# Moving the last feed-forward's norm, gate and first routing choice into the causal attention's slots (a four-block transformer stack on one Trainium2 core)

## The chip, the cores and the metric

The kernel runs on one core of a Trainium2 chip. A core has five engines with their own instruction queues: TensorE (PE, matrix products, with a separate row for its weight loads), VectorE (DVE), ScalarE (ACT), GpSimd (POOL) and SyncE (SP, which here only issues DMA transfers). SBUF is the on-chip memory, PSUM the banks that PE writes, DRAM the memory outside. The metric is the device time of one execution in microseconds (us); lower is better.

## The reference

The input is 8 rows of 512 tokens with 256 features. Six blocks are added to it one after the other, each on the layer norm of the running sum x:

```python
x = x + 0.5 * _L0_ffn_ref(_layernorm(x), ...)
x = x + _L0_attn_ref(_layernorm(x), ...)
x = x + 0.5 * _L0_ffn_ref(_layernorm(x), ...)
x = x + 0.5 * _L1_ffn_ref(_layernorm(x), ...)
x = x + _L1_attn_ref(_layernorm(x), ...)
x = x + 0.5 * _L1_ffn_ref(_layernorm(x), ...)
```

The change touches the last three. `_L1_attn_ref` is causal attention with 16 heads of 16 features, whose scores are scaled by an embedding of the distance (clipped at 16). `_L1_ffn_ref` is a mixture of 8 experts with a shared expert beside them:

```python
scores = sigmoid(x @ gate_W) * route_scale
topk_scores, topk_idx = top_k(scores, 2)
topk_w = topk_scores / topk_scores.sum(-1)
h = gelu(x @ W1[e] + b1[e]);  y = h @ W2[e] + b2[e]     # for each expert e
out = sum over the two chosen e of topk_w * y  +  gelu(x @ Ws1 + bs1) @ Ws2 + bs2
```

## The kernel before

x stays in SBUF as eight tiles `c.x[b]`, one per row of 512 tokens, each as 4 groups of 128 tokens on the partitions. All data is fp32, and the profile counts two matmul records for each fp32 product.

**The mixture (`l1_ffn`, called as "f3" ahead of the attention and as "f4" behind it).** For each row, `norm` (L994) normalises the four groups on ACT into a tile `xn`, SP stores it to a DRAM tensor (`f_xn` in the profile), and POOL adds half the shared expert's last bias to x (L998). `turn` (L1005) transposes the row on PE in two halves, each copied from its bank into `xnT`; `gate` (L1013) multiplies `xnT` with the gate's weights into the logits `lg`. `share` is the shared expert: a product with `ws1` (L1024), a gelu into `hs` (L1027), two products with `ws2` (L1033), each added to x by DVE (L1037). It reads the same `xnT`, so five of these tiles are kept. `choose(h)` routes one half of the rows (h = 0: rows 0 to 3; h = 1: rows 4 to 7): a sigmoid on ACT (L1088), the two best experts, and each token's place in a list sorted by expert and padded to 39 tiles of 128 tokens. A long series of small DVE operations, one pair of counting products (L1113, L1114), eight groups of four products that build the table of tokens (L1209), and one for the bias (L1230) do it. `lists` works through the 78 tiles of both halves: POOL gathers 128 tokens by index out of `f_xn` (L1246, `xe`), PE transposes them (L1254), ACT copies the expert's weights (L1284, `we`), PE multiplies (L1272), ACT takes the gelu (L1278, `h`), PE multiplies again (L1262), DVE adds the bias (L1264) and SP stores the tile (`f_y`). `fetch` (L941) gathers a token's two results, and `add` (L950) adds them to x with their weights.

These functions are Python generators. Each `yield` ends a piece of work, and the caller interleaves the pieces: `together` steps several generators in turn, `step` one. The order so written is kept on PE, DVE, ACT and POOL; on SP, in this function, a scheduler places the transfers. A call first runs `rows` up to the gate of row 3, then `choose(0)` together with the rest of `rows` (rows 4 to 7 and the shares of rows 0 to 3), then `lists`, with the other four shares, `choose(1)` and a second stream beside it. For f3 that second stream brings rows 0 and 1 to the attention; for f4 it fetches and stores rows 0 to 3. The last fetches of f4 follow behind the lists.

**The attention (`l1_attn`).** `attend` writes out by hand the order of all five engines, SP among them, as a series of slots: 32 groups (8 rows of 4 groups of heads), 8 slots each, so row b begins at slot 32 b. In a slot PE forms one pair of score products for finding the maxima (L1569, L1574), and for the group 12 slots back the products to be weighed (L1647, L1654, L1659), which ACT turns by an exponential into `pt` (L1663); every other slot PE sums them with the values (L1677, `o`). The score banks ("s", three of them) are taken twice in a slot. Everything else uses one further bank, "mm": norm and projections of the coming row, and the end of the finished one. These are placed by the list `pieces` of slot offsets and by `put`. The end of a row is `inverse` (reciprocal of the sums), `over` (spread to all partitions by way of DRAM), `scale` (L1526), and twice `finish` (product with Wo, L1533) and `add` (L1541), at offsets 48 to 63, so that for row 7 it comes after the last scores. The rows 2 to 7 come in from f3 by `bring` and `take` in the slots ahead.

The names and lines of this section and of the profile are those of the kernel before.

Of the kernel before, what the change touches and what calls it, by code (L numbers as in the profile page):

```python
# [921 lines left out]
def l1_ffn(c, k_, tag, keep, cut_row, beside):  # L922
# [4 lines left out]

# [6 lines left out]
    xn_d = keep["dram"].tile([NTOK, D], F32, name=f"{tag}_xn")  # L934
# [19 lines left out]
    with ExitStack() as ctx:  # L954
        rp = ctx.enter_context(tc.tile_pool(name=f"{tag}_rows", bufs=2))
        rt = ctx.enter_context(tc.tile_pool(name=f"{tag}_turned", bufs=5))
        hp_ = ctx.enter_context(tc.tile_pool(name=f"{tag}_half", bufs=1))
        sp = ctx.enter_context(tc.tile_pool(name=f"{tag}_small", bufs=2))
        ep = ctx.enter_context(tc.tile_pool(name=f"{tag}_e", bufs=3))
        wp = ctx.enter_context(tc.tile_pool(name=f"{tag}_we", bufs=4))  # L960
        xp = ctx.enter_context(tc.tile_pool(name=f"{tag}_xe", bufs=5))
        ps4 = ctx.enter_context(tc.tile_pool(name=f"{tag}_ps4", bufs=4, space=PSUM))
        ps = ctx.enter_context(tc.tile_pool(name=f"{tag}_ps", bufs=2, space=PSUM))
        ps1 = ctx.enter_context(tc.tile_pool(name=f"{tag}_ps1", bufs=1, space=PSUM))
        mv = hp_.tile([P, NA, 2], F32, name="mv")
        rstd = hp_.tile([P, NA], F32, name="rstd")
        shift = hp_.tile([P, NA], F32, name="shift")
        lgs = [hp_.tile([P, COUNT[h], NE1], F32, name=f"lg{h}") for h in range(2)]
        part_of = [{}, {}]
        xn, xnT = {}, {}  # L970

        def bank():
            return ps4.tile([P, T], F32, name="m")


        def stats(b):
            for i in range(NT):
                st = sp.tile([P, 6], F32, name="st")
                nc.vector.bn_stats(out=st, in_=c.x[b][:, i, :])
                nc.vector.bn_aggr(out=mv[:, b * NT + i, :], in_=st)  # L980

        def deviations(b0, b1_):
            a = slice(b0 * NT, b1_ * NT)
            nc.scalar.activation(rstd[:, a], mv[:, a, 1], AF.Sqrt, bias=c.eps)
            nc.vector.reciprocal(out=rstd[:, a], in_=rstd[:, a])
            nc.vector.scalar_tensor_tensor(
                out=shift[:, a], in0=mv[:, a, 0], scalar=-1.0, in1=rstd[:, a], op0=ALU.mult, op1=ALU.mult
            )

        def norm(b):  # L990
            xn[b] = rp.tile([P, NT, D], F32, name="xn")
            for i in range(NT):
                n = b * NT + i
                nc.scalar.activation(  # L994
                    xn[b][:, i, :], c.x[b][:, i, :], AF.Identity, bias=shift[:, n : n + 1], scale=rstd[:, n : n + 1]
                )
            nc.sync.dma_start(xn_d[b * T : (b + 1) * T, :].rearrange("(i p) d -> p i d", p=P), xn[b])
            nc.gpsimd.tensor_tensor(c.x[b], c.x[b], k_.bs2.unsqueeze(1).to_broadcast([P, NT, D]), ALU.add)  # L998

        def turn(b, kc):  # L1000
            if kc == 0:
                xnT[b] = rt.tile([P, KC, T], F32, name="xnT")
            m = bank()
            for i in range(NT):
                nc.tensor.transpose(m[:, i * P : (i + 1) * P], xn[b][:, i, kc * P : (kc + 1) * P], c.ident)  # L1005
            (nc.scalar.copy if kc == 0 else nc.vector.tensor_copy)(xnT[b][:, kc, :], m)

        def gate(b):
            h = int(b >= cut_row)
            m = bank()[:, : NT * NE1]  # L1010
            for i in range(NT):
                for kc in range(KC):
                    nc.tensor.matmul(  # L1013
                        m[:, i * NE1 : (i + 1) * NE1], lhsT=xnT[b][:, kc, i * P : (i + 1) * P],
                        rhs=k_.gate_w[:, kc, :], start=(kc == 0), stop=(kc == KC - 1),
                    )
            i0 = (b - R[h].start) * NT
            nc.scalar.copy(lgs[h][:, i0 : i0 + NT, :], m.rearrange("p (i e) -> p i e", e=NE1))


        def share(b):
            m = bank()
            for kc in range(KC):
                nc.tensor.matmul(m, lhsT=k_.ws1[:, kc, :], rhs=xnT[b][:, kc, :], start=(kc == 0), stop=(kc == KC - 1))  # L1024
            del xnT[b]
            hs = hp_.tile([P, T], F32, name="hs")
            nc.scalar.activation(hs, m, AF.Gelu, bias=k_.bs1)  # L1027
            yield
            for i2 in range(2):
                m = bank()  # L1030
                for j in range(2):
                    i = 2 * i2 + j
                    nc.tensor.matmul(  # L1033
                        m[:, j * D : (j + 1) * D], lhsT=hs[:, i * P : (i + 1) * P], rhs=k_.ws2, start=True, stop=True
                    )
                xs = c.x[b][:, 2 * i2 : 2 * i2 + 2, :]
                nc.vector.scalar_tensor_tensor(  # L1037
                    out=xs, in0=m.rearrange("p (j d) -> p j d", j=2), scalar=0.5, in1=xs, op0=ALU.mult, op1=ALU.add
                )
                yield  # L1040

        def rows():

            stats(0)
            deviations(0, 1)
            norm(0)
            for b in range(1, cut_row):
                stats(b)
            deviations(1, cut_row)
            yield  # L1050
            for b in range(NB + 1):
                if b < NB:
                    turn(b, 0)
                    yield
                if b:
                    gate(b - 1)
                    yield b - 1
                if b < NB:
                    turn(b, 1)
                    yield  # L1060
                if b + 1 < NB:
                    if b < cut_row:
                        n = len(R[1])
                        for e in R[1][max(0, b - 1) * n // (cut_row - 1) : b * n // (cut_row - 1)]:
                            stats(e)
                    if b + 1 == cut_row:
                        deviations(cut_row, NB)
                    norm(b + 1)
                    yield
                if cut_row <= b < NB:  # L1070
                    yield from share(b - cut_row)

        def shares():
            for b in range(NB - cut_row, NB):
                yield from share(b)


        def choose(h):
            t, lg, n_, n0, tiles = part_of[h], lgs[h], COUNT[h], R[h].start * NT, TILES[h]
            wide = [P, n_, NE1]  # L1080
            a = slice(n0, n0 + n_)

            def new(name, shape, dtype=F32, own=False):
                return hp_.tile(shape, dtype, name=f"{name}{h}" if own or COUNT[0] != COUNT[1] else name)

            yield
            score = new("score", wide)
            nc.scalar.activation(score, lg, AF.Sigmoid)  # L1088
            nc.vector.tensor_scalar_mul(score, score, k_.rscale)
            revw = k_.rev.unsqueeze(1).to_broadcast(wide)  # L1090
            top = new("top", [P, 2, n_])
            hot = [new(f"hot_{k}_", wide) for k in range(2)]
            tmp = new("tmp", wide)
            left = score
            for k in range(2):
                nc.vector.tensor_reduce(out=top[:, k, :], in_=left, axis=AX.X, op=ALU.max)
                nc.vector.tensor_tensor(tmp, left, top[:, k, :].unsqueeze(2).to_broadcast(wide), ALU.is_equal)
                yield
                nc.vector.tensor_tensor(tmp, tmp, revw, ALU.mult)
                first = new(f"first_{k}_", [P, n_])  # L1100
                nc.vector.tensor_reduce(out=first, in_=tmp, axis=AX.X, op=ALU.max)
                yield
                nc.vector.tensor_tensor(hot[k], revw, first.unsqueeze(2).to_broadcast(wide), ALU.is_equal)
                yield
                if k == 0:
                    left = new("left", wide)
                    nc.vector.scalar_tensor_tensor(
                        out=left, in0=hot[0], scalar=-3e38, in1=score, op0=ALU.mult, op1=ALU.add
                    )
# [16 lines left out]
            )  # L1126

            yield

            def running(u, n, inner, name):  # L1130

                s = 1
# [753 lines left out]
```

## Time and profile before

| what | us |
|---|---|
| median of 3 runs (3315.8 to 3321.88) | 3318.16 |
| the profiled execution | 3327.53 |
| its span, from first to last instruction | 3325.7 |
| PE busy in the span | 2783.5 (84%) |
| DVE / ACT / POOL busy | 1593.6 / 1637.5 / 1657.5 |
| f3: from its first statistics to its first list tile | 2026 to 2140 |
| f3: its lists | 2140 to 2312 |
| attention, up to its last product | 2312 to 2975 |
| last row's end and f4 up to its first list tile | 2975 to 3108 |
| f4: first list / second list | 3108 to 3203 / 3203 to 3276 |
| f4: last fetches and stores | 3276 to 3326 |

The mean granted clock of PE over the span is 0.91 of full speed. A stage's share of busy time is an average; which engine sets a stage's length is read from the waits inside it. Idle time of an engine that nobody waits for costs nothing. Ends of matmuls are modelled, so that a matmul's row may reach a little over the start of the next.

### The profile page before, as it was taken

To read this page: it belongs to the slowest core of one execution; us is meant where nothing else is said; L and a number is where in the kernel's file an instruction comes from. 1 tells how busy PE (TensorE), PEld (TensorE's weight loads), DVE (VectorE), ACT (ScalarE), POOL (GpSimd) and SP (SyncE) were. 2 spreads that over 40 slices of the span, in tenths; PEclk is the share of its full clock that TensorE was granted. 3 is DMA by queue.
4 is the path that set the end of the run, shared out by engine and by line. 5 is a ranking of instruction groups with operands and counts; after the bars stand their busy time and mean duration, and the time that the engine had idled before them with its cause. 6 is when DMAs were issued, how large, how long until landed. Compare 5 with 4: busy or idle time off the path is not lost.

```text
span 3325.7 us, 53835 instructions
## 1 busy us (share of the span) xinstructions
PE 2783.5 (84%) x20313; PEld 1997.7 (60%) x20313; DVE 1593.6 (48%) x3764; ACT 1637.5 (49%) x2593; POOL 1657.5 (50%) x1285
## 2 busy tenths in 40 slices
PE   6599999888888887468999996887999999977872
PEld 5589898733343443368989885665555555545752
DVE  8311111177777777292111113675656565545653
ACT  4133333379998999342333333266444444433451
POOL 3244444378888888243444442255635453422366
PEclk9699999899999999788999996799899999986896
DMA  6599999523555666766999983153001010001264
GB/s 228 175 305 305 308 305 301 171 51 37 82 62 76 84 84 93 104 219 200 306 302 308 301 274 109 37 146 110 25 23 32 21 33 15 15 23 51 79 174 147
DMA packets 373490, 475.88 MB, mean 143 GB/s; under 512 B 93800, under 2 KB 334320, under 8 KB 356848
## 3 DMA queue, kind: packets, MB, share of 16 engines
q1 hardware_dynamic: 335024, 401.63, 43.0%
q0 software_dynamic: 38208, 70.81, 9.5%
q8 instruction: 161, 2.64, 0.3%
q14 instruction: 97, 0.79, 0.1%
HBM read 379.42 MB, written 88.47 MB: 141 GB/s over the span
## 4 chain that ended last, share of the span: by engine, by line
PE 41%; ACT 13%; DVE 10%; DMA 7%; issue 5%; POOL 3%; SPq 1%; ACTq 0%; DVEq 0%; POOLq 0%
PE hp L303 7%; PE yp L310 7%; ACT ub L666 4%; DMA band_d<-e 2%; ACT ud L666 2%; PE s L1569 2%; PE yp L1262 2%; PE o L1677 2%; PE s L1654 2%; DVE ub L655 2%; PE s L1647 2%; PE mm L1424 2%; PE yp L1272 2%; PE s L1574 1%; DMA xe<-f_xn,tok_i 1%
## 5 line engine op out<-in xcount | busy, mean ns | idle before, releaser
L307 ACT ACTIVATE hT<-hp,b1T 128x128 f32<-128x128 f32 x1024 | 375.5, 367 | 616.1 <-PE hp L303 583.5
L303 PE MATMUL hp<-xeT,w 128*128 128x128 f32 x4096 | 562.3, 281 | 23.8 <-DVE xeT L296 22.3
L303 PEld LDWEIGHTS hp<-xeT,w 128*128 128x128 f32 x4096 | 529.1, 193 | 68.7 <-DVE xeT L296 29.9
L661 POOL TENSOR_TENSOR ud<-dk,dq 128x2048 f32<-128x2048 f32 x128 | 533.6, 4199 | 68.6 <-PE do L677 36.6
L310 PE MATMUL yp<-w,hT 128*128 128x256 f32 x2048 | 507.4, 381 | 0.0
L312 DVE TENSOR_TENSOR y<-yp,b 128x256 f32<-128x256 f32 x128 | 54.4, 425 | 846.1 <-PE yp L310 546.5
L310 PEld LDWEIGHTS yp<-w,hT 128*128 128x128 f32 x2048 | 360.6, 191 | 32.7
L655 DVE SCALAR_TENSOR_TENSOR ub<-bk,relb,bq 128x512 f32<-128x512 f32 x512 | 345.1, 740 | 5.5 <-PE bo L677 5.5
L1663 ACT ACTIVATE pt<-s 128x1024 f32<-128x1024 f32 (+3 forms) x256 | 180.1, 705 | 281.6 <-PE s L1659 222.0
L666 ACT ACTIVATE ud<-ud 128x2048 f32<-128x2048 f32 x128 | 244.8, 1913 | 24.5 <-POOL ud L661 24.3
L666 ACT ACTIVATE ub<-ub 128x2048 f32<-128x2048 f32 x128 | 245.6, 1918 | 6.8 <-DVE ub L655 6.6
L286 POOL PARTITION_BROADCAST b<-b2r x128 | 82.0, 645 | 332.8 <-DVE y L312 312.8
L1246 POOL DMA_INDIRECT xe<-f_xn,tok_i x156 | 148.5, 952 | 194.3 <-PE tp L1254 96.6
L288 POOL DMA_INDIRECT xe<-xn_d,slots x128 | 129.1, 1008 | 223.5 <-PE xp L294 173.8
L314 POOL DMA_INDIRECT acc_d<-y,slots x128 | 205.8, 1608 | 68.9 <-DVE y L313 37.4
L1596 POOL TENSOR_SCALAR_AFFINE_SELECT d<-d 128x512 f32<-128x512 f32 x128 | 84.8, 662 | 291.8 <-DVE d L1586 291.3
L1586 DVE TENSOR_TENSOR d<-s,fac 128x320 f32<-128x320 f32 (+1 forms) x256 | 120.7, 472 | 218.4 <-PE s L1574 196.3
L1628 POOL TENSOR_TENSOR d<-d,nm 128x640 f32<-128x640 f32 (+1 forms) x128 | 153.6, 1206 | 62.0 <-DVE nm L1608 61.8
L1647 PE MATMUL s<-qm,kp 32*128 32x384 f32 (+2 forms) x768 | 141.0, 443 | 20.0 <-ACT pt L1663 13.5
L677 PE MATMUL bo<-ub,o_w_bond_out 128*32 128x512 f32 x1024 | 144.3, 635 | 10.7 <-ACT ub L666 10.7
L1284 ACT COPY we<-wall 128x768 f32 x156 | 129.5, 832 | 44.4 <-DVE xeT L1257 20.6
L677 PE MATMUL do<-ud,o_w_damage_out 128*32 128x512 f32 x1024 | 139.5, 616 | 10.0 <-ACT ud L666 10.0
(463 smaller groups left out, 5126.6 us busy)
## 6 DMA issues: line engine op xcount, KB each, us to landing
w<-in_L_ffn_w_dram SPq DMA_DIRECT2D x256, 1024.0 KB
f_y<-y SPq DMA_DIRECT2D x156, 128.0 KB
vb<-val_d SPq DMA_DIRECT2D x16, 1024.0 KB
pb<-band_d SPq DMA_DIRECT2D x32, 512.0 KB
xn_d<-xn SPq DMA_DIRECT2D x16, 512.0 KB
acc_d<-x SPq DMA_DIRECT2D x16, 512.0 KB
x<-acc_d SPq DMA_DIRECT2D x16, 512.0 KB
val_d<-vhalf SPq DMA_DIRECT2D x16, 512.0 KB
```

Of the source, the lines that this page charges most:

```text
L303: nc.tensor.matmul(hp[:, jj, :], lhsT=w1[:, kc, :].rearrange("c (j p) -> c j p", j=NJ0)[:, j, :], rhs=xeT[:, kc, :], start=(kc == 0), stop ...
L307: nc.scalar.activation(hT[:, j, :], hp[:, jj, :], AF.Gelu, bias=b1T[:, j, e : e + 1])
L310: nc.tensor.matmul(yp, lhsT=hT[:, j, :], rhs=w2[:, j, :], start=(j == 0), stop=(j == NJ0 - 1))
L314: nc.gpsimd.indirect_dma_start(out=acc_d[:, :], out_offset=bass.IndirectOffsetOnAxis(ap=slots[:, e : e + 1], axis=0), in_=y, in_offset=Non ...
L655: nc.vector.scalar_tensor_tensor(out=ub[:, j, :], in0=bk[:, d : d + T], scalar=relb[:, d : d + 1], in1=t["bq"], op0=ALU.add, op1=ALU.add,)
L661: nc.gpsimd.tensor_tensor(ud, win, t["dq"].unsqueeze(1).to_broadcast([P, 4, T]), ALU.subtract)
L666: nc.scalar.activation(m, m, AF.Gelu)
L677: nc.tensor.matmul(out[32 * j : 32 * (j + 1), :], lhsT=outw[name][:, k, :], rhs=m[:, j, :], start=(k == 0), stop=(k == 3),)
L1246: nc.gpsimd.indirect_dma_start(out=xe[n], out_offset=None, in_=xn_d[:, :], in_offset=bass.IndirectOffsetOnAxis(ap=part_of[h]["tok_i"][:, j ...
L1628: nc.gpsimd.tensor_tensor(d[:, i, :, lo:], d[:, i, :, lo:], pads["nm"][n % 2][:, i, :, x : x + 1].to_broadcast([P, 4, NEAR - lo]), ALU.add,)
L1647: nc.tensor.matmul(tile_[:, j, P:w_], lhsT=pads["k"][g][r, kb * P : (kb + 1) * P], rhs=grp[n]["qm"][r, (kb + 1) * P :], start=True, stop=True,
L1663: nc.scalar.activation(grp[n]["pt"][:, 2 * pair : 2 * pair + 2, :w_], tile_[:, :, :w_], AF.Exp)
```

## The change

`l1_ffn` no longer runs a whole feed-forward. It makes the tensors of one call and returns its pieces as an object, and its working memory is opened later by `open_pools`. Both calls are made ahead of the attention, so f4's pieces can be placed inside it.

- The rows 0 to 5 of f4 get statistics, norm, bias, turn and gate in slots of the attention (`more`). The norm uses the attention's tile `xn`; all turns are copied by ACT, the bias is added in four parts.
- `choose(0)` of f4 is stepped once a slot from slot 200 (`each`). Its products borrow a score bank, and the table is gathered from the bank at once (`F.prompt`).
- The last attention row's end (`rest`), the statistics to gate of rows 6 and 7, and `choose(1)` make one stream, stepped once in each of the first four list steps and twice in each later one. f4's lists begin at once behind the attention; the shares of all eight rows and the fetches run beside them.
- `gate` drops `xnT` (except for rows 6 and 7 of f4), and `share` fetches the row's `xn` again from DRAM and turns it again. This holds for f3 too. `f_xn` becomes one tensor for each half.
- Some tiles become smaller or fewer: the values' tiles hold 17 columns a head in place of 32, `raw` has one buffer, `turned` 2 (f3) or 3 (f4) in place of 5, and small tiles of `choose` are shared.

```diff
-            for i in range(NT):
-                clear.memset(v[:, i], 0.0)
-                clear.memset(v[:, i, :, BD : BD + 1], 1.0)
+            v = const.tile([P, NT, NH * VW + 32 - VW], F32, name=f"vp{n}")
+            for i in range(NT):
+                clear.memset(v[:, i, :], 1.0)
...
+    def share(b):
+        if b not in xnT:
+            xn[b] = F.rp.tile([P, NT, D], F32, name="xn")
+            nc.sync.dma_start(xn[b], stored(b))
+            yield
+            yield
+            for kc in range(KC):
+                turn(b, kc)
+                yield
...
+def run_lists(F, choices, work, second, pace):
+    for s in F.lists():
+        step(work)
+        for _ in range(pace(s)):
+            step(choices)
+        if s == F.tiles[0] - 4:
+            for _ in choices:
+                pass
+        if s > F.tiles[0] + 3:
+            step(second)
...
+            def more(put):
+                for s, b in ((96, 0), (160, 2), (224, 4)):
+                    for i, t in enumerate((-29, -28, -27, -26)):
+                        put(s + t, f4.stats, b, (i,))
+                    for i, t in enumerate((1, 1, 3, 4)):
+                        put(s + t, f4.stats, b + 1, (i,))
+                    put(s + 5, f4.deviations, b, b + 2)
+                    put(s + 6, f4.inverses, b, b + 2)
+                    for e, norms, turns, gate in ((b, (15, 16), (23, 24), 29), (b + 1, (25, 26), (32, 37), 38)):
+                        put(s + norms[0], f4.norm, e, (0, 1), a2.xn)
+                        put(s + norms[1], f4.norm, e, (2, 3))
+                        for i in range(NT):
+                            put(s + norms[1] + 1 + i, f4.bias, e, i)
+                        put(s + turns[0], f4.turn, e, 0)
+                        put(s + turns[1], f4.turn, e, 1)
+                        put(s + gate, f4.gate, e)
...
+            def each(s, bank):
+                if s >= 200:
+                    f4.bank = bank
+                    step(choices)
+                    f4.bank = a2.bank
...
+        def last_rows():
+            yield from a2.rest(f4.bank)
+            for b in (NB - 2, NB - 1):
+                f4.stats(b)
+                yield
+            f4.deviations(NB - 2, NB)
+            for b in (NB - 2, NB - 1):
+                f4.norm(b)
+                yield
+                for kc in range(KC):
+                    f4.turn(b, kc)
+                    yield
+                f4.gate(b)
+                yield
+            yield from f4.choose(1)
+
+        def shares():
+            for b in [0, 1, 2, 3, 6, 7, 4, 5]:
+                yield from f4.share(b)
...
+        with in_order(c):
+            run_lists(f4, last_rows(), shares(), rows_out(0, CUT), lambda s: 1 + (s > 0))
+            for _ in rows_out(CUT, NB):
+                pass
```

## The prediction

> **What bounds the kernel now.** I read first the busy table by stage. Its columns are the stretch in us from the span's start, its length, the busy time (with instruction count) of TensorE (PE), its weight loads, VectorE (DVE), ScalarE (ACT) and GpSimd (POOL), the granted PE clock, the DMA share and GB/s.
>
> ```profile
> 2026.00:2140.00 114.00, 83.40 (x324) 63.87 (x325) 57.93 (x188) 33.69 (x64) 24.18 (x14) 0.60 0.25 84
> 2140.00:2312.00 172.00, 135.87 (x778) 107.52 (x776) 111.46 (x327) 107.67 (x178) 91.25 (x103) 0.96 0.44 128
> 2312.00:2975.00 663.00, 618.78 (x5379) 348.31 (x5376) 400.99 (x802) 289.72 (x444) 300.31 (x332) 0.94 0.08 23
> 2975.00:3108.00 133.00, 87.40 (x337) 66.54 (x338) 56.82 (x178) 32.31 (x64) 23.41 (x13) 0.62 0.12 41
> 3108.00:3203.00 95.00, 83.09 (x508) 67.35 (x507) 66.80 (x198) 63.16 (x105) 50.35 (x54) 1.00 0.49 139
> 3203.00:3276.00 73.00, 48.63 (x228) 38.03 (x226) 37.19 (x87) 33.38 (x57) 49.78 (x53) 0.84 0.59 172
> 3276.00:3326.00 50.00, 0.00 (x0) 0.00 (x0) 15.57 (x33) 0.00 (x0) 30.26 (x32) 0.54 0.46 139
> ```
>
> Row 3 is the causal attention: PE is busy 619 of 663 us, so PE work added there is paid. Row 4 is the last feed-forward's preparation (f4): 133 us before its first list tile, at clock 0.62. Then come its first list, its second list and the last rows' gathers. Rows 1 and 2 are the same feed-forward ahead of the attention (f3).
>
> Next the chain of waits through row 4 (start, us, what):
>
> ```profile
> 2979.59 1.72 DMA sums<-raw
> ...
> 2984.22 4.49 DMA rs<-inv_d
> 2988.83 1.24 DVE oc L1526
> 2990.11 3.64 PE mm L1533 x8
> ...
> 3011.27 3.21 PE m L1013 x16
> ```
>
> The last attention row ends in a bare latency: sums, inverse, DRAM and back, scaling at 2988.8, 14 us after the last attention matmul (2974.5). Then norm, turn and gate run at half clock: a gate takes 3.2 us.
>
> Third, the PE timeline, for prices at full clock and the pace of a list:
>
> ```profile
> 3048.26 0.60 PE L1005 MATMUL m<-ident,xn 128*128 128x128 f32 x4
> 3048.70 1.85 PE L1013 MATMUL m<-gate_w,xnT 128*128 128x8 f32 x16
> 3050.51 0.46 PE L1113 MATMUL m<-chosen,ones 128*128 128x128 f32 x2
> ...
> 3162.35 0.70 PE L1262 MATMUL yp<-we,h 128*128 128x256 f32 x2 [0.30 <-ACT h L1278]
> 3162.88 0.61 PE L1272 MATMUL yp<-xeT,we 128*128 128x128 f32 x4
> 3163.33 0.38 PE L1254 MATMUL tp<-ident,xe 128*128 128x128 f32 x2
> ```
>
> Start to start, a turn of half a row takes 0.44 us and a gate 1.8. A bare list step is 1.66 (3162.35 to 3164.01), of which about 1.1 is PE work and the rest the wait for h, which other work fills. The same view gives a share (ws1 1.71, ws2 twice 0.87) 3.45 us, and a choice 7.7: 0.5, eight table groups of 0.85, 0.4 for the bias.
>
> **Work moved into the attention's slots.** Rows 0 to 5: 6 x (2 x 0.44 + 1.8) = 16.1 us of PE, and the first choice 7.7, together 23.8; at the stage's clock of 0.94, 25 us. What is hidden beside PE: 24 norm tiles at 0.59 (14 us) and 12 bank copies at 0.58 (7) on ACT, busy 290 of 663; 24 statistics at 0.58 (14) and one choice, about 24 us by its groups, on DVE, busy 401; 24 bias tiles on POOL, a quarter of 2.35 each (14), busy 300. Without that cover DVE alone would cost 38. The six 512 KB stores go onto SP's queue ahead of the head gathers, which come once in eight slots (some 20 us): nothing. The new uses of the single "mm" bank fall on slots (5, 23, 24, 29, 0, 6 of each 32) that no other use takes; I allow 4 us for PE waiting on a late copy or add, against 13.6 us of such waits for L1541 now.
>
> The choice borrows a score bank ten times. Three banks rotate, two per slot, so a third user pulls the next slot's bank one step closer to its reader. Bounds: nothing, where DVE and ACT have already read it, and 0.5 us (the wait "PE s L1647 <- ACT pt L1663" shows 30 of at most 0.5): I take 0.4 x 10 = 4.
>
> **Activation tables and the clock.** Two of the three new square roots stand in slots 101 and 165, beside the attention's own, and share the table load. New are one square root (slot 229) and one sigmoid. The ACT timeline and the clock after such a switch:
>
> ```profile
> 2567.03 1.28 ACT L1399 ACT_TABLE_LOAD   x1
> 2568.32 0.30 ACT L1399 ACTIVATE rstd<-mv,eps 128x8 f32<-128x8 f32 x1
> 2568.64 1.28 ACT L1663 ACT_TABLE_LOAD   x1
> ...
> 2575.00:2579.00 4.00, 4.00 (x28) 2.34 (x28) 2.00 (x4) 0.98 (x2) 3.83 (x5) 0.50 0.00 0
> 2579.00:2583.00 4.00, 4.00 (x24) 2.10 (x20) 1.19 (x4) 0.38 (x1) 2.64 (x4) 0.50 0.02 4
> ```
>
> Two switches take ACT 2.6 us. The Trainium skill, "ScalarE: Activation LUTs", section "What ACT_TABLE_LOAD costs", adds a drain and has about 2.66 us for each; here the next activation starts 0.01 us after the load, so the row decides (by the rule, ACT would be held 5.3 us, and my sum would be 5 us higher over the two places). PE loses about 1.4 us of it, but then runs at half clock for some 15 us though it is busy all the time. "TensorE: Matmul & The Clock Gate", Part 1, has the clock back after about 3.4 us of sustained work, which would cost 1.7 us; the row costs 7. After two of the three present switches the clock fell (2399 and 2572, not 2742), so I take 1.4 + 2/3 x 7, about 6 each: 12. By the page it would be 6. Attention in all: 25 + 4 + 4 + 12 = **+45**, bounds +25 (moved work in gaps) and +90 (a half-clock stretch after each of seven or eight new stalls).
>
> **f3, which changes too.** Its gate now drops the turned row, so all eight shares fetch the row again (512 KB; "rs", 256 KB in two, landed in 4.5 us) and turn it: 16 x 0.44 = 7 us of PE. In row 1 four shares lengthen the work from 28 to 44 steps beside the 37 of the choice, so seven steps stand alone behind it (8 us at this stage's pace); against that, the choice's last table groups, now bare, are 0.9 us apart from waits on DVE, and filled (5 us). In the list half, turns fit into the waits for h, and a load has two list steps (3.3 us and more). The smaller "vp" saves four memsets of 0.2. Sum **+7**, bounds -8 and +23.
>
> **Behind the attention.** Gone from row 4: six rows' norm, turn, gate, and the first choice. The list starts at once, but three things stand in its way. SP has the reload of rows 0 and 1 around the last head gathers; POOL's first gather waits for those gathers to land (+7) and lands itself some 4 us later; and DVE carries the last row's inverse and scaling in order, ahead of xeT of list step 2, so PE stands behind scaling till about +17 (14 before, 3 for the reloads beside it). Of that time some 6 us of PE work is done. PE work to the end of the first list: 39 steps x 1.1 = 43; seven shares 24.2; twelve turns repeated 5.3; rows 6 and 7 4 x 0.44 + 2 x 1.8 = 5.4; the last row's two products 3.7; the second choice 7.7: 89. After +17, 83 are left. To this 3 us for the cold start and 12 for chains: square root, inverse, norm and turn of row 6 (6 us), row 7's norm behind row 6's store in the same buffer (4), two table loads. Bounds 0 (PE was busy 8.00 of 8 us in 3120:3128 under the same mix) and 30 (six reloads late by 3, hs waits of 0.84). So +115, where the same point stood at 3203 - 2974.5 = 228.5: **-113.5**.
>
> The second list is paced by POOL and DMA (PE busy 49 of 73) and hides the last share; the tail is POOL's and unchanged: 0, bounds 0 and +6.
>
> **Sum:** 45 + 7 - 113.5 = -61.5. The profiled execution took 3327.5 us (span 3325.7, 1.8 around it), so 3266; the median shown is 9.4 lower, so **3257 us**. Less than 0.2% (6.6 us) would not be told from no change.
>
> **Rivals.** (1) As summed, 0.72: 3225 to 3290. (2) The clock gives way in the attention: for it, half-clock stretches already follow small stalls, and the new banks and switches bring more; against it, the new work is full-array and PE stays busy. Full-clock work there is 663 less half of the 12% at half clock, 623, plus 24 = 647; with 32% of the time at half clock it takes 770, +107, and the gain is gone; from there it decides. At 40%: 809, +146, end 3318 + 146 + 7 - 113.5 = **3358**. 0.12. (3) The first list gets stuck on its reloads and chains and SP's order, so PE idles a third of it: 83 becomes 125, 3299 with the rest as summed; half of that, **3278**. For it, 18% of 3040:3065 was idle in the same kind of mixture. 0.10. (4) The attention takes the work in its waits and f3 gains by its fuller mix: 25 - 8 - 118: **3217**. Row 3 leaves only 44 us of PE not busy, so 0.06. That nothing moves is excluded: 130 us of work is taken out of row 4.
>
> Faster by over 0.2%: 0.72 + 0.10 + 0.06, less 0.03 for an end of (3) that just eats the gain, 0.85; within 0.03; slower, case (2), 0.12. The range leaves out most of (2) and the far end of (4): 3218 to 3308.
>
> **What would show it.** The gap between the last attention matmul and the first list's transposes falls from 133 us to some 12; the attention stage is 700 to 715 us with a clock near 0.92; the first list's stage takes about 100 us at clock near 1.0 with DVE's "oc" scaling as its first wait; the second list stays at 73 and the tail at 50. Wrong would be: an attention beyond 740, a list with PE below 75% busy, or f3 longer by over 25.

## The result: slower by 0.4%, and the profile after

The changed kernel takes 3333.68 us (median of 20 runs), the kernel before 3317.98 in the same series: ratio 1.0037, 95% interval 1.0020 to 1.0054. The prediction was 3257 us, a gain of 61, with a range of 3218 to 3308. The profiled execution took 3340.57 us (span 3338.8), 13.0 more than the one before.

The busy table by stage of the changed kernel has the same columns as in the prediction. Its rows are: f3 up to its first list tile, f3's lists, the attention, the time to f4's first list tile, f4's lists up to the first gather of the second stream, the rest of the lists, the tail.

```profile
2024.00:2141.00 117.00, 84.69 (x346) 65.94 (x347) 58.76 (x184) 32.31 (x64) 24.12 (x14) 0.58 0.30 98
2141.00:2325.60 184.60, 149.06 (x805) 118.59 (x802) 114.93 (x334) 113.54 (x187) 90.20 (x99) 0.90 0.43 125
2325.60:3060.80 735.20, 688.57 (x5606) 392.14 (x5606) 439.90 (x944) 314.78 (x494) 318.13 (x356) 0.87 0.09 25
3060.80:3071.50 10.70, 1.09 (x4) 0.72 (x4) 0.55 (x1) 3.28 (x4) 2.15 (x3) 0.50 0.40 127
3071.50:3202.20 130.70, 112.12 (x595) 90.80 (x596) 75.65 (x214) 66.40 (x112) 47.04 (x47) 0.87 0.40 114
3202.20:3289.00 86.80, 61.21 (x305) 48.06 (x303) 45.57 (x108) 43.64 (x74) 60.48 (x63) 0.88 0.60 172
3289.00:3338.80 49.80, 0.00 (x0) 0.00 (x0) 15.75 (x33) 0.00 (x0) 30.25 (x32) 0.51 0.46 140
```

The 133 us in front of f4's first list are gone: row 4 has 10.7. But the attention took 735 us in place of 663, and its clock fell from 0.94 to 0.87. From stage to stage (f3 is counted from its first statistics, the lists up to the first gather of the second stream, which stood at 3189.5 before):

| stage | before | after | difference | predicted |
|---|---|---|---|---|
| f3, to the attention's first score product | 284.6 | 301.7 | +17 | +7 |
| attention, to its last product | 663.4 | 735.2 | +72 | +45 |
| behind it, to the second stream's first gather | 215.0 | 141.4 | -74 | -113.5 |
| from there to the end | 136.2 | 136.6 | 0 | 0 |

The first three rows give +15; f3 also began 2.7 us earlier, together the 13 of the profiled executions.

The clock column says most. A gate took 1.8 us at full clock and 3.2 at half (both in the prediction's lines), so I take half of the time spent at half clock as lost; that time is "2 x (1 - clock) x length". The attention before: 0.12 x 663 = 80 us at half clock, 40 lost. After: 0.26 x 735 = 191, 96 lost. What is left of the stage without that loss is 623 and 640: +17. So by this estimate 55 of the 72 us are clock. It is an upper one: in the experiments below a us at half clock cost 0.38 to 0.49 us of the attention, which makes it 42 to 54.

Where the clock falls is seen in the changed kernel's PE timeline (start, us, what) and its busy table in steps of 4 us:

```profile
2678.92 1.06 PE L1727 MATMUL o<-pt,vp 128*32 128x512 f32 x8
2679.92 1.95 PE L1033 MATMUL mm<-gate_w,xnT 128*128 128x8 f32 x16
2681.80 0.41 PE L1619 MATMUL s<-kp,qp 32*128 32x160 f32 x2
```

```profile
2676.00:2680.00 4.00, 3.96 (x38) 1.98 (x37) 3.65 (x10) 3.31 (x6) 2.54 (x3) 1.00 0.18 50
2680.00:2684.00 4.00, 4.00 (x30) 2.80 (x30) 1.85 (x6) 0.19 (x1) 0.00 (x0) 0.77 0.20 51
2684.00:2688.00 4.00, 3.83 (x27) 2.06 (x26) 2.66 (x7) 2.49 (x5) 1.68 (x2) 0.50 0.00 0
...
2696.00:2700.00 4.00, 4.00 (x27) 2.09 (x28) 2.55 (x6) 1.24 (x2) 4.00 (x6) 0.50 0.00 0
2700.00:2704.00 4.00, 4.00 (x18) 1.45 (x16) 0.39 (x3) 1.02 (x3) 0.38 (x1) 0.67 0.00 0
```

This is the gate of row 1. It costs its 1.9 us, as priced. But PE was busy all through it and before it, and from its end the clock is at a half for 21 us. In steps of 1 us the six gates of the slots are followed by 8, 21, 7, 21, 8 and (up to the stage's end) 11 us of half clock: 76 us. In the 4 us before each of these stretches PE was not idle and no activation table was loaded. The trace's own record of the clock has only 0.5 and 1.0 in it, and each of its half-clock stretches is a multiple of 3.41 us: behind these gates 6.8, 20.5, 6.8, 20.5 and 6.8.

### The profile page after: what moved, and what is told of

The parts are those of the page before. It is cut to its first block, busy times and chain, and to the rows that moved or that the text cites. A ratio compares the mean times of both kernels' runs of the same rounds, so it can differ in the third digit from the quotient of the medians.

```text
span 3338.8 us, 54126 instructions
## 1 busy us (share of the span) xinstructions
PE 2822.8 (85%) x20425; PEld 2020.4 (61%) x20425; DVE 1597.7 (48%) x3770; ACT 1651.3 (49%) x2618; POOL 1660.2 (50%) x1299
## 5 line engine op out<-in xcount | busy, mean ns | idle before, releaser
L1275 POOL DMA_INDIRECT xe<-f_xn,f_tok x156 | 148.9, 954 | 208.7 <-PE tp L1283 134.3
L1697 PE MATMUL s<-qm,kp 32*128 32x384 f32 (+2 forms) x768 | 148.1, 464 | 16.8 <-ACT pt L1713 10.1
```

The source lines that it names most:

```text
L1275: nc.gpsimd.indirect_dma_start(out=xe[n], out_offset=None, in_=xn_d[h][:, :], in_offset=bass.IndirectOffsetOnAxis(ap=part_of[h]["tok_i"][: ...
L1697: nc.tensor.matmul(tile_[:, j, P:w_], lhsT=pads["k"][g][r, kb * P : (kb + 1) * P], rhs=grp[n]["qm"][r, (kb + 1) * P :], start=True, stop=True,
```

## The experiments

The totals are given as ratios to the kernel before on the same chip; its own median was between 3322 and 3375 us on the chips of these runs. On the slower ones the mixture stages stretch (f3 with unchanged code takes 283 to 298 us), the attention hardly (663.4 and 668.0 for unchanged code). Lengths of the attention, one profiled execution each, can therefore be set side by side; from repeats of nearly the same attention they scatter by some 10 us (735.2 and 722.8; 699.0, 697.7 and 691.9).

### Are the gates the cause?

**Gates out of the slots**, in the changed kernel:

```diff
-        m = F.bank()[:, : NT * NE1]
-        for i in range(NT):
+        if F.prompt:
+            m = k_.iota[:, : NT * NE1]
+        else:
+            m = F.bank()[:, : NT * NE1]
+        for i in range(0 if F.prompt else NT):
```

> The changed kernel without the gate products of rows 0 to 5 in the attention's slots: their logits are copied from a constant, so the first choice and the two lists work on other tokens than the reference's, while every other instruction stays. Theory G (the gates themselves take the clock): in the changed kernel's trace each of the six gates is followed by half clock, 8, 21, 7, 21, 8 and 11 us of it inside the attention, 76 us, which costs 38, and the products take 11 us; without them the attention falls from 735 to about 690 and the kernel from 3334 to about 3289. Rival S (the clock falls after any short stall of TensorE, and the slots are merely fuller): only the products' own 11 us go, 3322.

Measured: ratio 0.9943 (0.9921 to 0.9966), 0.94% below the changed kernel's or 31 us. The attention took 688.2 us at clock 0.93: 47 less, of which the products are 11. That is the length that theory G expected; the total fell by less than its 45 us. Most of that gap is scatter between executions: the profiled execution of the changed kernel was 7 us above its median, that of this run 6 below, and in the run further down whose attention is that of the changed kernel it took 722.8, not 735.2.

**Six idle gates in the kernel before**, with 8, 128 and 39 columns (w):

```diff
+            def more_pe():
+                m = ps.tile([P, T], F32, name="mm")
+                for i in range(NT):
+                    for kc in range(KC):
+                        nc.tensor.matmul(
+                            m[:, i * w : (i + 1) * w], lhsT=wt["Wq"][:, kc, i % 2 * P : (i % 2 + 1) * P],
+                            rhs=wt["Wk"][:, kc, :w], start=(kc == 0), stop=(kc == KC - 1),
+                        )
+                nc.scalar.copy(extra, m[:, :32])
+            for s in (96, 160, 224):
+                put(s + 29, more_pe)
+                put(s + 38, more_pe)
```

> The kernel before with six idle gates more in the same slots of its attention (16 products each of a 128x128 weight tile with 8 columns, copied out once by ScalarE and used by nobody). Theory G: 11 us of products and some 35 us of half clock behind them, so about 3364 against 3318. Rival S: 11 to 15 us, about 3331.

> As the run with six idle gates more, but with 128 columns in place of 8 in each product: as many products, as many weight loads, about the same time on TensorE. Theory G, that it is the few columns for each weight load which let the clock fall: no half clock behind them, about 3331. A rival, that any six further blocks of 2 us of work in these slots do it: the same 3364 as with 8 columns.

> The kernel before with six idle blocks more in its attention's slots, as the two runs before it, here with 39 columns for each weight tile, the width of the choice's table products. With 8 columns the attention took 691 us and each block had 7 to 21 us of half clock behind it; with 128 it took 667 and had none. Theory, that the share of time in which columns stream decides[...]: some blocks have a stretch of 4 us behind them, attention about 678, ratio 1.005. Rival, that only the very narrow product does it: 667, ratio 1.003.

(A block is 8 products, 16 records; the "16 products" of the first of these texts are the records.)

| columns | time of a block | attention | clock | ratio |
|---|---|---|---|---|
| none (two chips) | - | 663.4, 668.0 | 0.94, 0.93 | 1 |
| 8 | 1.95 | 691.1 | 0.91 | 1.0085 (1.0058 to 1.0113) |
| 39 | 1.98 | 667.7 | 0.95 | 1.0052 (1.0033 to 1.0071) |
| 128 | 2.05 | 666.9 | 0.95 | 1.0033 (1.0019 to 1.0048) |

The same block in the same slot, with 8 columns and then with 128; PE timeline and the stretches after it:

```profile
2839.64 1.95 PE L1741 MATMUL mm<-Wk,Wq 128*128 128x8 f32 x16
```

```profile
2842.00:2846.00 4.00, 3.83 (x26) 2.13 (x22) 1.95 (x4) 1.40 (x3) 0.63 (x1) 0.50 0.05 13
2846.00:2850.00 4.00, 4.00 (x29) 1.95 (x26) 1.12 (x4) 1.96 (x4) 1.10 (x2) 0.50 0.00 0
...
2858.00:2862.00 4.00, 4.00 (x19) 1.90 (x18) 1.75 (x3) 1.02 (x1) 1.12 (x2) 0.50 0.00 0
2862.00:2866.00 4.00, 3.93 (x37) 2.05 (x36) 1.02 (x2) 3.23 (x5) 0.64 (x1) 1.00 0.04 8
```

```profile
2841.71 2.05 PE L1741 MATMUL mm<-Wk,Wq 128*128 128x128 f32 x16
```

```profile
2844.00:2848.00 4.00, 3.52 (x40) 1.81 (x33) 2.56 (x6) 2.27 (x4) 1.19 (x2) 1.00 0.06 13
2848.00:2852.00 4.00, 4.00 (x49) 2.77 (x46) 2.47 (x6) 2.08 (x5) 3.32 (x5) 1.00 0.00 0
2852.00:2856.00 4.00, 4.00 (x32) 1.92 (x32) 2.49 (x5) 1.41 (x2) 4.00 (x5) 1.00 0.00 0
```

With 8 columns there are 8, 7, 5, 21, 8 and 7 us of half clock at the six blocks; with 128 or 39 columns none begins within 8 us of a block. So it is neither the added work nor the slots. The 8-column gates cost 17 us more than dense blocks of the same length by the ratios and 24 by the attention's length; I had expected 35, so the mechanism was right and its size in this kernel too high (the ratio, 1.0085 or 28 us, lies between theory G's 46 and rival S's 11 to 15). At 39 columns the trace speaks for the rival: no stretch behind a block, 667.7 us. The ratio does not decide it: 1.0052 is the theory's number, its interval reaches down to the 1.0033 of the dense blocks, and up into that of the 8-column ones.

**The gates turned round**, in the changed kernel. The gate's weights are stationary and the 512 tokens stream; the 8 rows of logits are turned back a slot later:

```diff
+    def gate_wide(b):
+        m = F.bank()[:NE1, :]
+        for kc in range(KC):
+            nc.tensor.matmul(
+                m, lhsT=k_.gate_w[:, kc, :], rhs=xnT[b][:, kc, :], start=(kc == 0), stop=(kc == KC - 1)
+            )
+        lgT[b] = xnT[b][:NE1, 0, :]
+        nc.scalar.copy(lgT[b], m)
...
+    def gate_back(b):
...
+        for i in range(NT):
+            nc.tensor.transpose(
+                m[:, i * NE1 : (i + 1) * NE1], lgT[b][:, i * P : (i + 1) * P], c.ident[:NE1, :NE1]
+            )
```

> The changed kernel with the six gates of the attention turned round: the gate's weights (8 columns) are the stationary side and the 512 tokens stream, two products for a row; the 8 rows of logits are copied and turned back a slot later in a borrowed score bank. Theory G: work on TensorE about the same (1.7 and 0.2 in place of 1.8), the half clock behind the gates gone: 3334 less some 35, about 3298. A rival, that it is the part of the array that works (8 of 128 columns in both forms): about 3336.

Measured: 0.9972 (0.9955 to 0.9988), 0.65% or 22 us below the changed kernel, and below the kernel before. The attention's row in the busy table:

```profile
2339.60:3038.60 699.00, 652.83 (x5558) 365.26 (x5558) 440.89 (x944) 318.04 (x500) 319.17 (x356) 0.93 0.10 27
```

It is 36 us shorter with as much work, and the half-clock time falls from 191 to 98 us; no stretch begins within 6 us of a turned gate, where behind the gates of 8 columns each began within 1 us. The gate's row above reads "128*128 128x8": the old form fills the whole array with weights and streams 8 columns (the expectation has this wrong). The turned form fills 8 of the array's 128 columns and streams 512. If the part of the array that works decided, the turned form would have been the worse one, so the rival is out. By the totals the form of the gates costs 17 to 22 us (this run; the two runs with blocks), by one profiled execution each 24 to 36.

### What does the first choice cost in the slots?

**The first choice out of the slots**, run alone between attention and lists, with the gates turned round:

```diff
             def each(s, bank):
-                if s >= 200:
-                    f4.bank = bank
-                    step(choices)
-                    f4.bank = a2.bank
...
         with in_order(c):
+            for _ in f4.choose(0):
+                pass
             run_lists(f4, last_rows(), shares(), rows_out(0, CUT), lambda s: 1 + (s > 0))
```

> The version with the gates turned round, and the first choice taken out of the attention's slots and run alone between the attention and the lists. Theory: in the slots the choice costs 7.7 us of products, some 3 of stalls and 18 for 37 us of half clock, so the attention falls from 699 to about 670, while the choice alone costs some 38 us in front of the lists: ratio about 1.000. Rival, that the choice's products are all it costs in the slots: attention 690, ratio 1.006.

Measured: 0.9990 (0.9971 to 1.0010). The busy table of this kernel, for the attention and the stretch up to the first list tile:

```profile
2362.30:3031.90 669.60, 626.84 (x5488) 349.60 (x5488) 411.51 (x856) 314.30 (x496) 317.60 (x356) 0.96 0.10 28
3031.90:3074.40 42.50, 18.31 (x75) 16.40 (x75) 23.34 (x89) 4.90 (x7) 2.21 (x3) 0.51 0.10 32
```

The choice costs 29 us in the slots (699.0 less 669.6), of which 7.7 are products and half of the 44 us by which the half-clock time differs (98 and 54) is 22. The sigmoid with its table load is part of the choice here. Alone the choice costs 32 (42.5 less 10.7). The slots hide almost nothing of it; the totals agree in so far as 0.9990 and 0.9972 are not told apart. On the other hand the six rows' turns and gates, 16 us of dense work, lengthen the attention by only 2 to 6 us over the unchanged one, in one profiled execution.

Two attempts at the choice's 22 us, both on the version with the gates turned round, failed. **One slot more** between the chosen experts and their counting products:

```diff
         nc.vector.tensor_tensor(chosen, hot[0], hot[1], ALU.add)
+        if F.prompt:
+            yield
         m = F.bank()[:, : 2 * n_ * NE1].rearrange("p (w i e) -> p w i e", w=2, e=NE1)
```

> The version with the gates turned round, and one slot more between the first choice's last comparison and its two counting products. In that version TensorE waits 0.98 us for DVE's "chosen" in the slot and then runs 15 us at half clock. Theory: a stall of 1 us can take the clock for 15 us, so 1 + 7.5 us go: ratio to the kernel before about 0.995, where the version without this edit had 0.997; attention 699 to about 691. Rival: half clock there comes from the mixture of work and not from this stall: 1 us, 0.997.

Measured: 0.9975 (0.9955 to 0.9994). The stall of 0.98 us and the half clock right behind it are gone (the products stand at 2918.75, no half clock from there until 2950), but two stretches of 17 us come later and the attention took 711 us. **The table products turned round**, for the choice in the slots alone; its table is turned back once at the end:

```diff
+            if F.prompt:
+                m = F.bank()[:tiles, :P]
+                for j in range(n):
+                    nc.tensor.matmul(m, lhsT=value[:, j, :], rhs=sits[:, j, :], start=(j == 0), stop=(j == n - 1))
...
```

> The version with the gates turned round, and the first choice's table products in the attention's slots turned round as well: 128 columns stream against 39 stationary ones, in place of 39 against 128, and the table of 39x128 is turned back once at the end. Theory, that few columns for each weight load let the clock fall here too: in the changed kernel 4 us of half clock follow several of the eight groups; without them some 8 to 12 us go, attention 699 to about 689, ratio 0.994 (0.997 without this edit). Rival: 39 columns are enough to keep the clock, and the stretches near the groups come from stalls: 0.997 to 0.998.

Measured: 0.9993 (0.9974 to 1.0012), attention 698.0: no gain in the total. But the trace does not bear the rival out. The 30 us from just ahead of the counting products, with the table products as they were and turned round:

```profile
2876.00:2906.00 30.00, 28.85 (x208) 16.38 (x208) 19.06 (x55) 11.01 (x17) 7.30 (x8) 0.77 0.10 28
2903.00:2933.00 30.00, 27.03 (x246) 15.34 (x246) 23.87 (x62) 12.51 (x19) 7.94 (x9) 1.00 0.10 28
```

In the second row PE waits just as long for "chosen" (0.99 us), and no half clock follows, so this stall alone does not take the clock. The short stretches behind the table groups are gone as well: from the sigmoid to the end of the choice the half clock falls from 37 to 17 us. The attention is no shorter because PE waits 5 us more in it (51 in place of 46), and because one of its own square roots has 14 us of half clock behind it in place of 3. What in the choice takes the clock stays open: the stall is not enough, the table products may have a part.

### What holds the first list?

The waits of PE in the first list of the changed kernel (us in all, times, longest):

```profile
PE m L1239 <- DVE value L1235: 7.5, 5, 3.1
PE tp L1283 <- DMA xe<-f_xn,f_tok: 5.7, 1, 5.7
PE yp L1291 <- ACT h L1307: 3.6, 7, 1.9
...
```

The first line is the second choice. Its table groups are asked for once in a list step, some 4 us apart. Each needs only 1.5 us of DVE (0.7 for "sits", 0.6 for "value", 0.2 for the table; the expectations below speak of 4), but "value" stands in DVE's order behind the add of a share, which itself waits for PE's product of that list step. The second line, the first gather, was foreseen in the prediction: POOL issued it 8 us behind the attention, when the last row's reciprocal was done.

**The second choice left out**, in the changed kernel:

```diff
+    def same_choice():
+        for name in ("off_i", "tok_i", "b1t"):
+            nc.vector.tensor_copy(part_of[1][name], part_of[0][name])
...
-            yield from f4.choose(1)
+            f4.same_choice()
+            yield
```

> The changed kernel with the second choice left out: rows 4 to 7 are given the places of rows 0 to 3, so the second list does other tokens than the reference's; its lists have as many tiles. Theory: behind the attention the miss is the second choice's pace: its 7.7 us of products, 9 us in which TensorE waits for its DVE steps (value, pick, chosen) and some 7 for the half clock behind these waits, 24 us in all: about 3310, ratio 0.997; the second stream's first gather at 118 us behind the attention in place of 141. Rival: the first list is held by reloads, gathers and the gelu's waits, so only the products go: about 3326, ratio 1.001.

Measured: 0.9950 (0.9932 to 0.9968), 29 us below the changed kernel; second stream's first gather 114.9 us behind the attention (141.4 with the choice). The wait for "value" is of course gone, and the clock there is 0.91. (The first list tile also came earlier, 4.9 us behind the attention in place of 10.7. That gained under 1 us: PE still stood behind the last row's scaling until 17.5, with the same work done as before.)

**A slower pace for its end**, with the gates turned round:

```diff
-            run_lists(f4, last_rows(), shares(), rows_out(0, CUT), lambda s: 1 + (s > 0))
+            run_lists(f4, last_rows(), shares(), rows_out(0, CUT), lambda s: 1 + (0 < s < 19))
```

> The version with the gates turned round, and the second choice stepped twice in a list step only up to step 18, once from there on, so that its table groups (about 4 us of DVE each) have two list steps in place of one. Theory: TensorE's waits for DVE's "value" (7.5 us, five times) and the 15 us of half clock behind them go, some 12 us: second stream's first gather at about 130 us behind the attention in place of 142, ratio 0.994. Rival: the choice is on the way to the second list in any case, and the steps only move its end: 0.997, with the last groups bunched before the second list.

Measured: 0.9932 (0.9907 to 0.9958), the gather at 131.6 us (141.9 without this edit). The same line of the waits:

```profile
PE m L1259 <- DVE value L1255: 3.1, 1, 3.1
```

So the choice was not "on the way in any case": of the 19 us that it takes beyond its products, 10 were pace. With both edits the changed kernel beats the one before, by 0.7%.

### f3, and the gates there

**The reload alone**, in f3 of the kernel before:

```diff
             nc.scalar.copy(lgs[h][:, i0 : i0 + NT, :], m.rearrange("p (i e) -> p i e", e=NE1))
+            if tag == "f3":
+                del xnT[b]
...
         def share(b):
+            if b not in xnT:
+                xn[b] = rp.tile([P, NT, D], F32, name="xn")
+                nc.sync.dma_start(xn[b], xn_d[b * T : (b + 1) * T, :].rearrange("(i p) d -> p i d", p=P))
+                yield
+                yield
+                for kc in range(KC):
+                    turn(b, kc)
+                    yield
```

> The kernel before with one part of the change alone: in the feed-forward ahead of the attention, the gate drops the turned row, and the shared expert fetches and turns it again. Theory: this carries what that feed-forward grew by, 7 us of turns and some 12 by clock and waits: ratio 1.005. Rival: the work fits into the list's waits and the rest of the growth came from elsewhere: 1.000 to 1.002.

Measured: 1.0065 (1.0044 to 1.0086), 22 us. f3 took 313.1 us. Unchanged f3 took 296.6 and 298.3 on another chip of nearly that speed, the changed one 311.5 to 315.2 on these chips. So the reload is f3's growth, within the scatter of some 4 us; the other 6 us of the total are not placed.

**All gates of f3 turned round too**, on top of the slower pace (`gate` in `rows` becomes `gate_wide` and `gate_back`, a step apart):

> The version with the gates of the attention turned round and the slower pace of the second choice, and in addition the eight gates of the feed-forward ahead of the attention turned round, which run in its row stage at a clock of 0.59. Theory: where TensorE is idle for a third of the time anyway the clock is lost to that idle time and not to the gates, so nothing is gained: row stage 117 us as now, ratio 0.993 as without this edit. Rival: the gates hold the clock down there too, and the stage gets shorter by some 8 us: 0.991.

Measured: 0.9918 (0.9891 to 0.9945), not to be told from 0.9932. The row stage took 118.6 us (117.0 without this edit), though its clock rose from 0.59 to 0.69: PE is not what that stage waits for. This version has the lowest ratio, 0.8% below the kernel before.

## Why the prediction was wrong

By the profiled executions the sum was 75 us too low: 27 in the attention, 10 in f3 and 40 behind the attention, of which 13.5 are a wrong mark. The plan itself held: the 133 us ahead of the list became 10.7. None of the prediction's three signs of being wrong came (735 is below 740, PE was busy 86% of the list, f3 grew by less than 25): the misses were spread over three stages.

**Attention, +45 predicted, +72 measured.** The sum had two parts: work and waits, 25 + 4 + 4, and the clock, 12. Without the clock loss the stage grew by 17 to 30, no more than the 33; the time in which PE was not busy grew from 44 to 47 us, so the waits cost about 3 and not 8. The step that failed is "Activation tables and the clock": half clock was priced only behind the new table switches, 12 us, and behind the gates and the choice's products at nothing. The switches were small: in the changed kernel the new square root has some 5 us of half clock behind it, and the sigmoid falls into a gate's stretch. The clock cost 42 to 55 us. By the lengths of the attention in the runs, the 72 are 36 for the form of the gates (735.2 to 699.0), 29 for the choice, 22 of them clock (to 669.6), and 2 to 6 for all the rest.

The prediction had the loss of the clock in its rival (2), and there argued it away: "the new work is full-array and PE stays busy". Both are true of the gates, and the clock fell all the same. The gate's row was shown in the prediction, "128x8 f32 x16": 1.85 us busy for 8 columns a product. That is the time of its weight loads: their row is busy 1.93 of the 1.95 us of a block with 8 columns, and 1.93 of 2.05 with 128. Busy did not mean that columns streamed. The rival's own sum put the point of no gain at a half-clock share of 32%; it came to 26% and needed the two misses below to go over the line. The Trainium skill, "TensorE: Matmul & The Clock Gate", Part 1, says that a monitor of PE's activity sets the clock over a free-running window of about 3.4 us. The multiples of 3.41 us in the trace's clock record agree with that. By the page one busy window is enough to release the clock again; here PE was busy through six (the rows of the 21 us above) and stayed at half. What the monitor counts no run here shows.

**f3, +7 predicted, +17 measured.** The sum was loose (its terms, 7 + 8 - 5 less 0.8, give 9), and the step "A load has two list steps" and "turns fit into the waits for h" was too kind: reload and turns alone made f3 some 15 us longer. The wait for h fell only from 18.5 to 17.3 us, so the turns were paid beside it, and, as the list's clock of 0.96 before and 0.90 after suggests, partly at half clock.

**Behind the attention, -113.5 predicted, -74 measured.** The start was right: PE stood behind the last row's scaling until 3078.88, 18 us behind the attention's last product (17 predicted):

```profile
3060.14 0.65 PE L1727 MATMUL o<-pt,vp 128*32 128x128 f32 x8 [0.47 <-ACT pt L1713]
3064.77 1.09 PE L1025 MATMUL m<-ident,xn 128*128 128x128 f32 x4 [3.98 <-DMA xn<-f_xn]
3071.52 0.69 PE L1283 MATMUL tp<-ident,xe 128*128 128x128 f32 x2 [5.66 <-DMA xe<-f_xn,f_tok]
...
3078.88 3.72 PE L1518 MATMUL m<-Wo,oc 128*128 128x256 f32 x16 [0.62 <-DVE oc L1511]
```

Of the 40 us missing, 13.5 are a wrong mark: "the same point stood at 3203" was not the same point. The second stream's first gather stood at 3189.5 before, so +115 would have been a gain of 100. For the other 26 (the gather came at 141.4 and not 115) the step that failed is the second choice: it was entered with its products, 7.7, and its steps on DVE at nothing, while "12 for chains" held only the norms of rows 6 and 7 and two table loads. It takes 26.5 there, by the run without it, 19 more than was entered. Of that, 10 went with the slower pace. The last 7 stay open; in the run without the choice the clock still loses half of 0.18 x 115, an estimated 10 us, against 3 "for the cold start".

**Second list and tail, 0:** right (136.2 and 136.6).

## What to carry to other kernels

Before you move a small matmul into a stage that PE bounds, look at how many columns stream for each weight load: six gates of 8 columns, 11 us of work, cost 28 us where they were added and 31 to 47 where they were taken out; turned round they gave 22 to 36 us back, and blocks of the same length with 128 columns cost their own 11 us by the totals and less by the attention's length. Between 8 and 39 columns nothing was measured. Price an edit to such a stage as "work and waits" plus "time at half clock", and read the second from 4 us steps of the busy table right behind every new kind of instruction, in whatever stage it stands now. When two versions are compared at a mark inside a pipeline, take one named instruction that both have.

## What the runs showed that was not expected

- Blocks of eight products of 8 columns and of 128 take nearly the same time (1.95 and 2.05 us), but only the first let the clock fall: half clock follows each of the 12 blocks and gates of 8 columns, and none of the 12 blocks of 39 or 128. By the trace 39 columns behave like 128; the totals leave it open.
- In the profiled executions dense work in the slots was almost free: 11 us of it left the attention at 667 us, between the two unchanged ones (663 and 668), at a higher clock (0.95 against 0.93 and 0.94). The total shows no such gain (1.0033 is its 11 us), so this may be scatter.
- Half clock at the same place of the program returned with nearly the same lengths: in the clock record 6.8, 20.5, 6.8, 20.5, 6.8 us behind the first five gates of the changed kernel, 6.8, 17.1, 6.8, 20.5, 6.8 in the run without the second choice, and 6.8, 6.8, 3.4, 20.5, 6.8 behind the blocks added to the kernel before.
